# The order of row blocks in a whole-sum pass, and the place of its first eight rows

## The chip, the cores and the metric

The kernel runs on one core of one Trainium2 chip. A run's time is in device microseconds (us); lower is better. The kernel before was run three times. One more execution was taken with the hardware profiler, and all views of the profile come from it.

The engines are named by the profile's letters: PE is TensorE (PEld its weight loads), DVE is VectorE, ACT is ScalarE, POOL is GpSimd, and SP is the sync engine, whose queue issues most of the DMA transfers.

## The reference

The input is a feature matrix x of 2708 nodes by 128, and a 2708 by 2708 float32 matrix `adj`. Four layers follow, each of the form "layer norm of x plus a graph layer". Only the first two matter here:

```python
# layer 0
A_hat = adj + I;  d = A_hat.sum(1) ** -0.5
x = layernorm(x + (d[:, None] * A_hat * d[None, :]) @ x @ W.T + b)
# layer 1
XW = x @ W;  s_col = XW @ a[:f];  s_row = XW @ a[f:]
den = exp(leaky_relu(s_row[:, None] + s_col[None, :], 0.01))
num = adj @ den
att = where(num != 0, den / num, 0)
x = layernorm(x + adj @ (att @ XW))
```

The other two layers (a hyperbolic one, and one with the masks adj > 0 and adj < 0) come later and are not touched.

## The kernel before

The matrix comes in transposed, as `adjT`. It is cut into `NT` = 22 row tiles of 128 rows (the last has 20) and `NB` = 6 blocks of up to 512. Blocks 0 to 3 hold 4 tiles and 512 columns each; block 4 has 4 tiles too; block 5 has 2 tiles and 148 columns. A tile `A{d}_{c}` or `B{d}_{c}` holds row block d and column block c; a full one is 1 MB (1024 KB), one of the last column block 296 KB.

**Layer 0** streams all of adjT once as A tiles, adds up the degrees, and multiplies. Some tiles remain in SBUF (`kept`), in eleven "places" and some "thin" buffers for the narrow last column block. After the degrees, a loop over column blocks c = 0 to 4 finishes the layer. One pass of it issues, on TensorE, in a fixed order:

- `last_products`: the products with row blocks 4 and 5 for block c (`a`, L866; the unit matrix, L914), in three parts. Between the parts stand `norm_roots(c-1)` (the sums of squares, `var`, L251, then three ACT steps and DVE's split in three terms, `work`, L267) and `normed(c-1)` (a spread of the roots, `rs`, L273, then DVE's multiplication into `x`, L992).
- `projected(c-1)`: the products `xw` with the weights of layer 1 (L1001), then ACT copies `rc` and `xw`, and a store of `xw_d` on SP's queue (L1012).
- `degree_rows(c+1)`: `db`, L244, and ACT's copy.
- `summed_up(c)`: DVE adds up the block (L962, L963), ACT squares it (L965).
- `clamped(c-1)` and `count(c-1)`: DVE clamps the scores (`rcl`, L1019) and compares them with samples, eight `counts` (L1051) a full block, four for block 5. ACT also makes `e1`, the exponential of the score, from the clamped scores, block by block.

The same steps for blocks 4 and 5 follow after the loop; this is the tail of layer 0. `queued(engine)` ties each block of instructions behind the latest one queued on that engine, so the written order is kept there.

**The sort before layer 1.** Layer 1's numerators aren't computed as one large product: nodes are sorted into groups by score, and the numerator of a group is the one before it, changed by the nodes of that group. The stage needs `below` (sums of the counts, L1190), three transposes `prev_ps` (L1223), 26 DVE steps `jk` that follow each other (L1239), six broadcasts `rb` (L238) with ACT's `q_b`, the matmuls `low` (L1288, L1298), and two lists (`ohs` on DVE, L1326, `list` on PE, L1328). POOL then gathers rows of adjT (`rows_g`, L1415), and the attention loop begins (`num`, L1464).

**The whole-sum pass.** The first numerator is the sum over all rows k of e1[k] times row k of adjT. `whole_sum(n)` does the next n row tiles of it ("rows" from here on) into two PSUM banks (`t`, L803; the accumulators are `tot`). A row is nine matmuls with one output partition each, 18 records in the trace, over four column groups:

```python
sums_of = [(c, 0, BW, 32 * c, 0, 0) for c in range(4)]
sums_of += [(4, i * q4, min(BW, (i + 1) * q4), 32 * i, 1, 0) for i in range(4)]
sums_of += [(5, 0, width(5), 96, 1, BW - 3 * q4)]
```

Row blocks 4 and 5 are still in SBUF from layer 0. Row blocks 0 to 3 are fetched again, as B tiles, in that order: `fetch_next()` issues the loads on SP's queue (L824) for as long as `free_places` has a place. Seven places are free at first, which serves block 0 (places 6, 9, 3, 7 and 10) and B1_0 and B1_1 (place 1, and a buffer in `ut`). When the last row of a block has been summed, its places go back to the list and `fetch_next()` is called again. The thin buffer of B2_5 is that of A4_5, so this load must wait for block 4's rows in any case.

The rows were taken in the block order 0, 4, 5, 1, 2, 3. They were issued by calls of `sum_rows(n)`: four of them in the tail of layer 0, ten around `prev_ps` and `rb`, two ahead of the first list and one each at its steps 8 and 16, two ahead of the second list. At the end ACT copies the totals into `carry0`, two rows that POOL cleared before (L1166), in a region that the xw_d stores read.

Of the kernel before, what the change touches and what calls it, by code (L numbers as in the profile page):

```python
# [25 lines left out]
NB = (N + BW - 1) // BW  # L26
# [18 lines left out]
def rows(t):  # L45
    return min(P, N - t * P)


def width(b):
    return min(BW, N - b * BW)  # L50


def tiles(b):
    return range(b * (BW // P), min(NT, (b + 1) * (BW // P)))
# [3 lines left out]
def kernel(  # L58
# [20 lines left out]
    nc = tc.nc  # L79
# [98 lines left out]
    def acc_tile(b, name):  # L178
        return psum.tile([P, BW], F32, tag=f"acc{b}", name=name)

    def ps_tile(name):
        return psum.tile([P, BW], F32, tag="ps", name=name, bufs=2)
# [24 lines left out]
    def bslice(b):  # L207
        return slice(b * BW, b * BW + width(b))
# [555 lines left out]
    def fetch_next():  # L764

        while True:
            if not waiting:
                waiting.extend(itertools.islice(fetches, 1))
            if not waiting:
                return  # L770
            d, c = waiting[0]
            if c == NB - 1:
                t = thin_place((0, 1, 2, 0)[d], f"B{d}_{c}")
            elif free_places:
                held.setdefault(d, []).append(free_places.pop(0))
                t = big_place(held[d][-1], f"B{d}_{c}")
            else:
                return
            waiting.pop()
            kept[d, c] = fill_tile(t, d, c)  # L780
# [4 lines left out]
    e1 = c_tile("e1")  # L785
    e2 = c_tile("e2")
    q4 = (N - 4 * BW) // 4
    order = [0, NB - 2, NB - 1, *range(1, NB - 2)]
    steps = iter([(d, i) for d in order for i in range(len(tiles(d)))])

    sums_of = [(c, 0, BW, 32 * c, 0, 0) for c in range(4)]
# [4 lines left out]
    def whole_sum(n):  # L796
        if not tot:
            tot.extend(acc_tile(i, f"t1_{i}") for i in range(2))
        for d, i in itertools.islice(steps, n):
            k = tiles(d)[i]  # L800
            kw = rows(k)
            for c, a, b, o, bank, at in sums_of:
                last = nc.tensor.matmul(  # L803
                    tot[bank][o : o + 1, at : at + b - a],
                    lhsT=e1[:kw, k : k + 1],
                    rhs=kept[d, c][:kw, i, a:b],

                    start=(k == 0 and at == 0),
                    stop=(d == order[-1] and i == 3),
                    skip_group_check=True,  # L810
                )
            if i == len(tiles(d)) - 1:
                if d == NB - 2:
                    free_places.extend([4, 8, 0, 5, 2])
                elif d < NB - 2:
                    free_places.extend(held.pop(d))
                fetch_next()
        return last

    def fill_tile(t, d, c):  # L820
        w = width(c)
# [19 lines left out]
    with tc.tile_pool(name="tri", bufs=1) as tp:  # L841
# [115 lines left out]
        def summed_up(c):  # L957

            w, cs = width(c), bslice(c)
            dw, s, sq = (works[c][:, i, :w] for i in range(3))  # L960
            with queued(DVE):
                nc.vector.tensor_mul(s, acc[c][:, :w], dw)  # L962
                nc.vector.scalar_tensor_tensor(s, s, b0_s, x[:, cs], op0=ALU.add, op1=ALU.add)  # L963
            with queued(ACT):
                nc.scalar.activation(sq, s, AF.Square)  # L965
# [94 lines left out]

        def sum_rows(n):
            with queued(PE):
                return whole_sum(n)

        scaled = None

# [60 lines left out]
        for c in range(NB - 1):  # L1127
            for part in range(3):
                last_products(c, part)
                if c and part == 0:  # L1130
                    norm_roots(c - 1)
                    if c > 1:
                        count(c - 2, 4, 7)
                elif c and part == 1:
                    normed(c - 1)
                    if c > 1:
                        count(c - 2, 7)
            if c:
                projected(c - 1)
                degree_rows(c + 1)  # L1140
            summed_up(c)
            if c:
                clamped(c - 1)
                count(c - 1, 0, 4 if c < NB - 2 else 1)
# [2 lines left out]
        count(NB - 3, 1, 3)  # L1147
        norm_roots(NB - 2)
        norm_roots(NB - 1)
        sum_rows(1)  # L1150
        count(NB - 3, 3, 6)
        normed(NB - 2)
        sum_rows(1)
# [1 line left out]
        count(NB - 3, 6)  # L1155
        projected(NB - 2)
        projected(NB - 1)
        sum_rows(2)
        clamped(NB - 2)
        count(NB - 2)  # L1160
        clamped(NB - 1)
# [6 lines left out]
    with ctx_keep:  # L1168
# [11 lines left out]
        with tc.tile_pool(name="sort", bufs=1) as st_p:  # L1180
# [36 lines left out]
                    )  # L1217
            nc.vector.tensor_tensor(prev[:, 0, :], prev[:, 0, :], prev[:, 1, :], op=ALU.max)
            prev_ps = ps_tile("prev_ps")
            sum_rows(2)  # L1220
            with queued(PE):
                for q in range(len(SAMPLES)):
                    nc.tensor.transpose(  # L1223
# [1 line left out]
                    )  # L1225
            for b in range(NB):
                w, cs = width(b), bslice(b)
                sum_rows(3 if b < 2 else 1)
                with queued(PE):
                    pr = bcast_block(rcl[:, 0, :], b, f"rb{b}")  # L1230
                with queued(ACT):
                    nc.scalar.activation(q_b[:, cs], pr[:, :w], AF.Exp, scale=0.99)
# [75 lines left out]
            for i in range(2):  # L1308
                for n in range(3):
                    nc.vector.tensor_mul(  # L1310
                        val[i][:, :, 2 + n, :], oh[i], terms[:, n, i, :].unsqueeze(2).to_broadcast(grid)
                    )
                for h, (ta, tb) in enumerate(((0, t_a), (t_a, NT))):
                    nn = (tb - ta) * GM
                    nc.vector.tensor_mul(
                        pos[i][:, ta:tb, :], low[i, h][:, :nn].rearrange("p (t g) -> p t g", g=GM), oh[i][:, ta:tb, :]
                    )
                nc.vector.tensor_reduce(slot[:, i, :], pos[i], AX.X, ALU.add)
                nc.vector.tensor_scalar(slot[:, i, :], slot[:, i, :], 2.0, None, op0=ALU.add)
                ps = ps_tile(f"list{i}")  # L1320
                sum_rows(2)
                for t in range(NT):
                    if i == 0 and t in (8, 16):
                        sum_rows(1)
                    ohs = srt([P, P], f"ohs{i}_{t}", BF16, 10, "ohs")
                    nc.vector.tensor_scalar(ohs, iota_b, slot[:, i, t : t + 1], None, op0=ALU.is_equal)  # L1326
                    with queued(PE):
                        nc.tensor.matmul(  # L1328
                            ps[:, : 6 * GM],
                            lhsT=ohs,  # L1330
                            rhs=val[i][:, t, :, :].rearrange("p n g -> p (n g)"),
                            start=(t == 0),
                            stop=(t == NT - 1),
                        )
                lists.append(ps[:, : 6 * GM].rearrange("p (n g) -> p n g", g=GM))
                li = srt([P, 6, GM], f"list_s{i}")
                nc.vector.tensor_copy(li, lists[i])
                node, value, occ = li[:, 0, :], li[:, 2, :], li[:, 5, :]
                nc.vector.scalar_tensor_tensor(node, node, float(P), li[:, 1, :], op0=ALU.mult, op1=ALU.add)
                if i == 0:  # L1340
                    for h in range(2):
                        fi = srt([P, GM], f"fi{h}", F32, 2, "fi")
                        nc.vector.tensor_scalar(fi, node, 2.0, float(h), op0=ALU.mult, op1=ALU.add)
                        nc.vector.tensor_scalar(row_i[:, h, :], fi, 0.0, float(2 * N - 1), op0=ALU.max, op1=ALU.min)
                else:
                    nc.vector.tensor_scalar(inval, occ, -1.0, 1.0, op0=ALU.mult, op1=ALU.add)
                    nc.vector.scalar_tensor_tensor(node, inval, float(N), node, op0=ALU.mult, op1=ALU.add)
                    nc.vector.tensor_scalar(xw_i, node, 0.0, float(N), op0=ALU.max, op1=ALU.min)

                nc.vector.tensor_add(value, value, li[:, 3, :])  # L1350
                nc.vector.tensor_add(value, value, li[:, 4, :])
                mask = srt([P, GM], f"mask{i}")
                nc.vector.tensor_scalar(mask, occ, -EMPTY, EMPTY, op0=ALU.mult, op1=ALU.add)
                nc.vector.tensor_add(value, value, mask)
                if i == 0:
                    nc.scalar.activation(e1_l, value, AF.Exp)
                    nc.scalar.activation(e2_l, value, AF.Exp, scale=0.01)
                else:
                    nc.scalar.activation(gj_l, value, AF.Exp, scale=0.99)
                    nc.vector.tensor_copy(occ_l, occ)  # L1360

                    nc.vector.tensor_scalar(inval, inval, 1.0e-18, None, op0=ALU.max)
# [615 lines left out]
```

## Time and profile before

| | us |
|---|---|
| median of 3 runs (lowest, highest) | 903.19 (901.72, 904.63) |
| the profiled execution | 905.07 |
| its span, first to last instruction | 903.4 |
| PE busy | 847.1 |
| DVE busy | 554.8 |
| ACT busy | 389.0 |
| POOL busy | 206.1 |

The span is what the instruction records cover; 1.67 us of the profiled execution lie outside it. The granted TensorE clock had a mean of 0.973 of full speed. An engine's busy time says how much it did, not what the end waited for: this is told by the chain of waits, by the timeline of a stretch, and by the table of windows (busy time, granted clock and DMA rate in a stretch). Times in a timeline count from the span's start.

### The profile page before, as it was taken

To read this page: it belongs to the slowest core of one execution; us is meant where nothing else is said; L and a number is where in the kernel's file an instruction comes from. 1 tells how busy PE (TensorE), PEld (TensorE's weight loads), DVE (VectorE), ACT (ScalarE), POOL (GpSimd) and SP (SyncE) were. 2 spreads that over 40 slices of the span, in tenths; PEclk is the share of its full clock that TensorE was granted. 3 is DMA by queue.
4 is the path that set the end of the run, shared out by engine and by line. 5 is a ranking of instruction groups with operands and counts; after the bars stand their busy time and mean duration, and the time that the engine had idled before them with its cause. 6 is when DMAs were issued, how large, how long until landed. Compare 5 with 4: busy or idle time off the path is not lost.

```text
span 903.4 us, 9470 instructions
## 1 busy us (share of the span) xinstructions
PE 847.1 (94%) x3268; PEld 429.5 (48%) x3268; DVE 554.8 (61%) x1189; ACT 389.0 (43%) x681; POOL 206.1 (23%) x176
## 2 busy tenths in 40 slices
PE   3699999699899999999999999989999899999996
PEld 3244454335344445444454444534444555555555
DVE  4777548988788888889971226375644564233313
ACT  3776433215787777787761115273332221000000
POOL 5221000101788885776500000000000000000000
PEclk9799999989899999999999999999999999999997
DMA  9995684596596555445534776496764565474410
GB/s 341 366 361 204 120 245 144 182 383 215 180 372 213 151 162 158 142 153 154 154 122 168 266 268 229 134 335 238 265 222 132 210 211 198 145 253 142 160 42 19
DMA packets 95979, 184.30 MB, mean 204 GB/s; under 512 B 6446, under 2 KB 23551, under 8 KB 95668
## 3 DMA queue, kind: packets, MB, share of 16 engines
q1 hardware_dynamic: 85700, 143.82, 46.2%
q0 software_dynamic: 8352, 37.76, 13.0%
q10 hardware_dynamic: 1872, 2.04, 0.7%
q8 instruction: 28, 0.46, 0.2%
q14 instruction: 27, 0.22, 0.1%
HBM read 179.33 MB, written 4.28 MB: 203 GB/s over the span
## 4 chain that ended last, share of the span: by engine, by line
PE 84%; DMA 8%; DVE 5%; ACT 2%; issue 1%; SPq 0%; DVEq 0%; ACTq 0%
PE a L1588 22%; PE num L1464 13%; PE uacc L1491 13%; PE a L1867 12%; PE a L866 10%; PE a L1876 6%; DMA A<-in_adjT_dram 4%; DMA B<-in_adjT_dram 3%; PE t L803 1%; DMA cb<-in_adjT_dram 1%; PE pp L1825 1%; DVE counts L1051 1%; PE mx L1695 1%; PE su L251 0%; DVE work L267 0%
## 5 line engine op out<-in xcount | busy, mean ns | idle before, releaser
L1415 POOL DMA_INDIRECT rows_g<-in_adjT_dram,row_i x52 | 131.2, 2523 | 90.6 <-PE num L1464 40.9
L1469 ACT ACTIVATE ln<-num,inval,occ_l 128x512 f32<-128x512 f32 x156 | 107.5, 725 | 52.7 <-DVE rows_g L1467 48.7
L1867 PE MATMUL a<-cb,ut 128*128 128x512 f32 (+2 forms) x264 | 125.8, 559 | 1.3 <-DMA cb<-in_adjT_dram 1.3
L1491 PE MATMUL uacc<-att,xw_g 128*128 128x512 f32 (+1 forms) x312 | 126.3, 542 | 0.0
L1876 PE MATMUL a<-mask,node 128*128 128x512 f32 (+2 forms) x264 | 120.3, 537 | 0.7 <-DVE mask L1855 0.7
L1464 PE MATMUL num<-rows_g,w_all 128*128 128x512 f32 (+1 forms) x276 | 113.6, 544 | 0.8 <-ACT ln L1469 0.8
L1588 PE MATMUL a<-cb,q_b 128*128 128x512 f32 (+2 forms) x264 | 111.7, 561 | 1.8 <-DMA cb<-in_adjT_dram 1.8
L866 PE MATMUL a<-A,q_b 128*128 128x512 f32 (+2 forms) x264 | 106.1, 549 | 1.5 <-DMA A<-in_adjT_dram 1.5
L1588 PE MATMUL a<-cb,xw 128*128 128x512 f32 (+2 forms) x264 | 107.3, 550 | 0.0
L1467 DVE COPY rows_g<-num 2x512 f32<-2x512 f32 x150 | 88.0, 612 | 15.8 <-PE num L1464 14.6
L1491 PEld LDWEIGHTS uacc<-att,xw_g 128*128 128x128 f32 x312 | 59.1, 190 | 59.1 <-issue 50.0
L1483 DVE TENSOR_TENSOR att<-att,ln 128x1354 f32<-128x1354 f32 x52 | 80.5, 1548 | 2.0 <-ACT ln L1479 2.0
L1464 PEld LDWEIGHTS num<-rows_g,w_all 128*128 128x128 f32 x276 | 49.8, 190 | 53.8 <-issue 39.6
L1876 PEld LDWEIGHTS a<-mask,node 128*128 128x128 f32 (+1 forms) x264 | 48.5, 193 | 49.4 <-issue 47.6
L230 ACT ACTIVATE sq_l<-s 128x512 f32<-128x512 f32 (+1 forms) x11 | 6.6, 604 | 148.4 <-DVE s L1885 116.7
L1479 ACT ACTIVATE ln<-ln 128x1354 f32<-128x1354 f32 x52 | 69.3, 1333 | 1.7
L1855 DVE TENSOR_SCALAR mask<-cb 128x3072 fp32r<-128x3072 f32 (+5 forms) x24 | 33.5, 1395 | 59.3 <-PE a L1876 58.6
L866 PEld LDWEIGHTS a<-A,q_b 128*128 128x128 f32 (+1 forms) x264 | 45.9, 191 | 50.0 <-issue 46.7
L1588 PEld LDWEIGHTS a<-cb,q_b 128*128 128x128 f32 (+1 forms) x264 | 45.1, 192 | 46.9 <-issue 42.8
L1588 PEld LDWEIGHTS a<-cb,xw 128*128 128x128 f32 (+1 forms) x264 | 45.1, 190 | 46.5 <-issue 46.5
L1074 ACT ACTIVATE xw<-A 128x2048 f32<-128x2048 f32 (+3 forms) x36 | 57.0, 1582 | 8.3 <-DMA b_s<-in_b_dram 4.4
L1456 DVE TENSOR_SCALAR att<-q_b,gj_l 128x1354 f32<-128x1354 f32 x52 | 48.2, 927 | 12.6 <-PE uacc L1491 12.5
(445 smaller groups left out, 899.5 us busy)
## 6 DMA issues: line engine op xcount, KB each, us to landing
cb<-in_adjT_dram SPq DMA_DIRECT2D x15, 2816.0 KB
cb<-in_adjT_dram SPq DMA_DIRECT2D x15, 2560.0 KB
A<-in_adjT_dram SPq DMA_DIRECT2D x25, 1024.0 KB
B<-in_adjT_dram SPq DMA_DIRECT2D x18, 1024.0 KB
cb<-in_adjT_dram SPq DMA_DIRECT2D x3, 814.0 KB
cb<-in_adjT_dram SPq DMA_DIRECT2D x3, 740.0 KB
ut<-in_adjT_dram SPq DMA_DIRECT2D x2, 1024.0 KB
A<-in_adjT_dram SPq DMA_DIRECT2D x5, 296.0 KB
```

Of the source, the lines that this page charges most:

```text
L866: nc.tensor.matmul(acc[c][:, :w], lhsT=z[:kw, k, :], rhs=t[:kw, i, :w], start=c not in begun, stop=(d == NB - 1 and k == NT - 1), skip_gro ...
L1074: checks[d, c] = nc.scalar.activation(below[:, :nt, :w], t[:, :nt, :w], AF.Relu, scale=-1.0, accum_out=neg_sum[:, NB * c + d : NB * c + d ...
L1415: got = nc.gpsimd.indirect_dma_start(out=gat[q], out_offset=None, in_=adj_h, in_offset=bass.IndirectOffsetOnAxis(ap=row_i[:, h, g : g + 1] ...
L1464: nc.tensor.matmul(num[:, : cb - ca], lhsT=w, rhs=gat[q][:, ca:cb], start=True, stop=True)
L1467: nc.vector.tensor_copy(gat[q + 1][0:2, ca:cb], num[0:2, : cb - ca])
L1469: nc.scalar.activation(ln_n[q][:, ca:cb], num[:, : cb - ca], AF.Ln, scale=occ_l[:, g : g + 1], bias=inval[:, g : g + 1],)
L1479: nc.scalar.activation(ln_n[q], ln_n[q], AF.Exp, scale=-1.0)
L1483: nc.vector.tensor_mul(att[q], att[q], ln_n[q])
L1491: nc.tensor.matmul(uacc[h][c][:, : cb - ca], lhsT=xw_g[:, g, :], rhs=att[q][:, ca:cb], start=(g == 0), stop=(g == GM - 1),)
L1588: nc.tensor.matmul(acc[:, :w], lhsT=weights[:kw, k, :], rhs=pc[:kw, t, :w], start=(k == 0), stop=(k == NT - 1),)
L1867: nc.tensor.matmul(acc[:, :w], lhsT=edge[:ke, k, :], rhs=pc[:ke, t, :w], start=(k == 0), stop=False, skip_group_check=True,)
L1876: nc.tensor.matmul(acc[:, :w], lhsT=node[:kw, k, j, :], rhs=mask[:kw, t - ma, :w], start=False, stop=(k == NT - 1 and j == 1), skip_group_ ...
```

## The change

The order of row blocks becomes 0, 1, 4, 5, 2, 3. The places of block 1 are thus given back before those of block 4, and the later loads take other places and follow in another order. The calls of `sum_rows` are set anew: two rows each in the passes c = 3 and c = 4 of the loop (all of block 0), right behind `degree_rows(c+1)` on TensorE's queue; two, one and one in the tail (all of block 1); one ahead of `prev_ps` and eight in the first four `rb` steps (block 4, block 5, three rows of block 2); three ahead of the first list, and one each at its steps 8 and 16 (the last of block 2, and block 3); none ahead of the second list. `whole_sum` no longer returns its last instruction, which no caller used.

```diff
-    order = [0, NB - 2, NB - 1, *range(1, NB - 2)]
+    order = [0, 1, NB - 2, NB - 1, *range(2, NB - 2)]
...
-                last = nc.tensor.matmul(
+                nc.tensor.matmul(
...
-        return last
...
-                return whole_sum(n)
+                whole_sum(n)
...
             summed_up(c)
+            if c in (NB - 3, NB - 2):
+                sum_rows(2)
             if c:
                 clamped(c - 1)
...
         norm_roots(NB - 1)
-        sum_rows(1)
+        sum_rows(2)
         count(NB - 3, 3, 6)
         normed(NB - 2)
         sum_rows(1)
...
         projected(NB - 1)
-        sum_rows(2)
+        sum_rows(1)
         clamped(NB - 2)
...
             prev_ps = ps_tile("prev_ps")
-            sum_rows(2)
+            sum_rows(1)
...
-                sum_rows(3 if b < 2 else 1)
+                sum_rows(2 if b < 4 else 0)
...
                 ps = ps_tile(f"list{i}")
-                sum_rows(2)
+                sum_rows(3 if i == 0 else 0)
```

In the order that the build gives the instructions, TensorE has the rows at the places named. SP's queue issues B1_2, B1_3, B1_4, B2_0 and B2_1 ahead of the last two xw_d stores; then B2_2, B2_3 (in `ut`), B2_4, B3_0, B3_1, B2_5 and the rest of block 3; the store of `x_d` (L1518, 1408 KB), which stood ahead of these loads, comes last. On POOL the clearing of `carry0` comes ahead of the four small `terms` steps, which stood before it. On ACT `e1_l` comes behind six of the nine copies into `carry0`, and on DVE the copy of `carry0` into the first gathered rows comes ahead of the two copies into `w_all`.

## The prediction

> **What bounds the kernel now.** I read the page first: engine shares and the chain that ended last.
>
> ```profile
> PE 847.1 (94%) x3268; PEld 429.5 (48%) x3268; DVE 554.8 (61%) x1189; ACT 389.0 (43%) x681; POOL 206.1 (23%) x176
> PE 84%; DMA 8%; DVE 5%; ACT 2%; issue 1%; SPq 0%; DVEq 0%; ACTq 0%
> ```
>
> TensorE bounds the kernel as a whole, but the edit lies between 150 and 225 us, so that stretch decides. TensorE's timeline there (start, duration, instruction, idle before it):
>
> ```profile
> 150.65 1.16 PE L1001 MATMUL xw<-w1ext,x 128*128 128x130 f32 x8
> 151.65 0.60 PE L244 MATMUL db<-ident,dcol 128*128 128x128 f32 x4
> 152.09 1.06 PE L914 MATMUL a<-ident,q_b 128*128 128x128 f32 x8
> ...
> 157.43 0.40 PE L273 MATMUL rs<-work,sel 128*128 128x128 bf16 x4 [0.29 <-DVE work L267]
> ...
> 165.75 0.40 PE L273 MATMUL rs<-work,sel 128*128 128x128 bf16 x4 [0.43 <-DVE work L267]
> 166.08 1.34 PE L803 MATMUL t<-B,e 128*1 128x512 f32 x18
> 167.35 0.28 PE L273 MATMUL rs<-work,sel 64*128 64x128 bf16 x2
> 168.88 1.61 PE L1001 MATMUL xw<-w1ext,x 128*128 128x130 f32 x12 [1.24 <-DVE x L992]
> 170.42 2.50 PE L803 MATMUL t<-B,e 128*1 128x512 f32 x36
> 177.61 0.48 PE L1190 MATMUL below<-counts,ones_b 128*128 128x384 bf16 x1 [4.69 <-DVE counts L1051]
> ```
>
> Two regimes. In the block loop (143.5 to 161.0) TensorE is busy 16.92 of 17.5 us (window table), and the gaps of 0.29 wait for VectorE work that TensorE's own earlier "var" matmul started: a TensorE loop. After 163 VectorE rules: the sum rows (L803) fill waits, and TensorE idles 4.69 us for the counts. Four rows there cost nothing today.
>
> Then the waits, and SP's timeline:
>
> ```profile
> PE below L1190 <- DVE counts L1051: 4.7, 1, 4.7
> PE t L803 <- DMA B<-in_adjT_dram: 2.2, 2, 1.7
> SPq L824 <- PE t L803: 7.9, 2, 7.3
> ```
> ```profile
> 169.07 0.33 SPq L1518 DMA_DIRECT2D x_d<-x  x1
> 170.54 1.77 SPq L1012 DMA_DIRECT2D xw_d<-xw  x2
> 172.60 24.06 SPq L824 DMA_DIRECT2D B<-in_adjT_dram  x12
> ```
>
> The next B loads leave at 172.60, once row block 0 is summed and its places are free. From the window table (start:end, length, busy time of PE, PEld, DVE, ACT, POOL, granted clock, DMA share, GB/s):
>
> ```profile
> 143.50:152.00 8.50, 8.21 (x42) 3.95 (x41) 7.88 (x26) 3.39 (x13) 0.19 (x1) 1.00 0.11 34
> 182.00:183.00 1.00, 1.00 (x14) 0.20 (x6) 0.13 (x1) 0.00 (x0) 0.00 (x0) 0.50 1.01 381
> 184.00:188.00 4.00, 4.00 (x62) 1.92 (x58) 3.79 (x12) 0.09 (x1) 0.00 (x0) 1.00 1.05 384
> 200.00:201.00 1.00, 0.89 (x4) 0.40 (x5) 0.93 (x5) 0.00 (x0) 0.00 (x0) 0.54 1.06 389
> ```
>
> DMA is nearly idle to 168, then saturated at about 385 GB/s. TensorE's clock is half after each pause.
>
> **What the skill says.** The Trainium skill, "DMA: Bandwidth & Descriptors", section "Anatomy of one DMA": [...]semaphore waits hold the issuing sequencer. [...]B2_4 released TensorE at 199.15; it and all queued ahead (eight B loads of 1.049 MB, x_d 1.44 MB, xw_d 0.39 MB: 10.2 MB) had by the window table (10.9 MB moved from 168 to 199.1) passed 1.7 us earlier. "TensorE: Matmul & The Clock Gate", Part 1: an idle window of about 3.4 us halves the clock, as long a busy one restores it. Here idleness from 172.9 gave 0.60 in 176 to 177 and 0.50 until 183; even the 1.7 and 0.5 us waits around 198 to 200 gave 0.54. Same page, Part 3: small-M matmuls to different 32-column groups run concurrently. Here 18 records of up to 0.59 us make a row of 1.25.
>
> **The change, part by part.** *Unit.* A row is 18 records; two rows took 2.50 us at 170.42, hence 1.25 each at full clock; at half clock two took 178.61 to 183.16, 4.55.
>
> *Block 0's rows move into passes c = 3 and c = 4* (two each, behind "db", ahead of the next pass). The built order has them there. Their loads landed long before (DMA idle from 144), so no wait. But TensorE sets the pace there, and var, ACT's roots and L267 all follow behind: 2 x 2.5 = **+5.0 us** with no cover. The four rows taken out of the tail save nothing: they lay under VectorE.
>
> *Block 1's rows come into the tail, with their loads.* B1_2, B1_3 and B1_4 need places of block 0, freed by its last row. In pass 4 "db" was 160.71 to 160.93; shifted 2.5, rows 163.4 to 165.9, the last from 164.7, its first matmuls done near 165.6: the loads leave then, 7.0 earlier than before. But block 1's first row now stands right behind the second "var", which ended at 164.2, so 169.2 now. Three loads are 3.15 MB: at 385 GB/s 8.2 us, plus 2.2 fixed (1.7 measured after the bytes, about 0.5 before them: x_d, issued at 169.07, showed bytes before 170). B1_4 lands at **176.0**. B1_0 and B1_1 are there early; each later matmul stops for its load: a wait of up to 6.8 us in pieces.
>
> *Who stands behind it.* In TensorE's queue: normed(4)'s spread (rs), a row, normed(5)'s rs, projected(4), (5), the last row; behind those ACT's rc, VectorE's rcl and 12 counts, then "below". VectorE can do only three counts of block 3 meanwhile; the last two stand behind x. After landing, two rows owe ten narrow matmuls: 0.85 us at full, 1.7 at half clock. So rs starts at 176.9 to 177.7 against 165.75. From rs to rcl took 4.52 (165.75 to 170.27), about 2 of it VectorE's counts, done by now. In its place TensorE does rs 0.4, row 1.25, rs 0.28, then xw to rcl 1.4: 3.4, or 3.8 with VectorE's last two counts after x of block 5, at full clock; up to 6.0 with matmuls doubled. The clock should be half; I take 4.9. Rcl: 177.3 + 4.9 = 182.2 against 170.27, **+11.9** (both ends: +10.4 to +13.4). From rcl to "below" VectorE's 7.34 stays: below at 189.5.
>
> *What comes back.* One row instead of two ahead of prev_ps: it ran at 183.16 though VectorE was ready at 182.12, -1.0. Later, loads that start earlier against a chain 12 us later have landed: the 2.2 us of B waits go, and the lists have five rows, not six, none ahead of the second. The 26 jk steps (184.3 to 201.4) stay VectorE's, so only VectorE's idle gaps between 213 and 222.5 can close: 0.66 + 0.53 + 0.30 + 0.34 = 1.8. Together 1.0 to 2.8; I take **-2.0**.
>
> *At nothing.* SP: the xw_d stores of blocks 4 and 5 now stand behind five B loads, x_d behind all. They hold the carry0 memset (2.44 us) and POOL's terms, moved behind it; that is done near 190, needed near 213. B2_5 shares A4_5's buffer, so it and block 3's last loads wait for block 4: in by about 212, wanted near 219. Were these covers gone, each would cost a wait like the 2.2 above. ACT's carry copies and VectorE's carry copy swap places with e1_l and w_all, which have slack (first matmul 227.50, carry done 226.5). The dropped return value issues nothing. The attention loop and later layers shift whole.
>
> *Sum.* +11.9 - 2.0 = **+9.9 us**. The profiled execution took 905.07 (span 903.4, 1.67 around it), 1.9 above the median of 903.19; I add to the median: **913.1**. Ends: 10.4 - 2.8 = +7.6, 13.4 - 1.0 = +12.4.
>
> **Rivals.** *Loads in time.* If no row stops for a load, rs is late by 5.0 alone and the return is 2.0: 906.2. This needs 3.15 MB plus the fixed part in the 3.6 us between 165.6 and 169.2; the fastest microsecond shows 439 GB/s. Were block 1's places free earlier it would hold; they are not. 7%.
> *Faster.* The inserted rows hide: VectorE idles 1.35 us for ACT in pass 4, and if the loop's real bound were VectorE or ACT, +5.0 becomes 0; with loads in time, only the return stays, at its full 2.8: 900.4. It decides where rcl is late by less than 2.8 minus the 2.7 that 0.3% needs, so practically not at all. Against it: TensorE's 16.92 of 17.5 us and that the 1.35 wait starts from a TensorE matmul. 3%.
> *Longer.* Half clock holds through the tail and again through the lists (TensorE would idle before "low" with fewer rows), the return is lost: up to 13.4 + 2 for doubled matmuls in the lists, 918.6. For it: 0.54 after a mere 2 us pause. 10%.
> *It doesn't do what it says.* A scheduler could put the rows elsewhere; the built order shows them where the text puts them, so only its waits are open.
>
> **How the numbers follow.** My case has 80%: 910.8 to 915.6 by its ends, widened by about 2 for the landing estimate. The range 907.5 to 917.0 leaves out the first two rivals, most of the third, and a small part of mine: under 2 in 10. 0.3% (2.7 us) is about what a measurement of this kernel can tell from no change. Faster by more 3%; within 5% (half of the first rival and a little of mine); slower 92%.
>
> **What would show it.** Right: L803 rows near 152 and 163; a TensorE wait of about 6 us on B between 169 and 176, then clock 0.5; "below" near 189.5; no B wait after 195; everything from L1464 on as long as before. Wrong: "below" before 184 (loads were fast), or the list's end, 44.9 us after "below" today (177.61 to 222.46), unchanged or longer (no return).

## The result, and the profile after

The kernel before ran in 903.88 us here (median of 4 runs), the changed kernel in 912.26 us (median of 4, 911.88 to 916.96). The ratio is 1.0109, with a 95% interval of 1.0071 to 1.0146: 6.4 to 13.2 us slower. Run once more, beside other kernels, it took 914.37 us (median of 5) against 902.77 (ratio 1.0136, 1.0111 to 1.0161). The profiled execution took 916.96 us, the slowest of the four; its span is 915.2 us. The other three took 911.88 to 912.43.

Engine shares and the chain that ended last:

```profile
PE 850.1 (93%) x3268; PEld 429.9 (47%) x3268; DVE 555.8 (61%) x1189; ACT 389.1 (43%) x681; POOL 204.0 (22%) x176
PE 84%; DVE 7%; DMA 6%; ACT 2%; issue 1%; DVEq 0%; SPq 0%; ACTq 0%
```

The same instructions, 3268 matmuls as before; TensorE's busy time grew by 3.0 us of the 11.8 that the span grew, so most of the loss is idleness. Below, a part of TensorE's work is called cold where the granted clock was half, and warm where it was full. TensorE's timeline (start, duration, instruction, idle before it; "below" is L1191 now, line numbers move by one or two):

```profile
152.05 2.50 PE L803 MATMUL t<-B,e 128*1 128x512 f32 x36
159.92 0.40 PE L273 MATMUL rs<-work,sel 128*128 128x128 bf16 x4 [0.29 <-DVE work L267]
163.52 2.50 PE L803 MATMUL t<-B,e 128*1 128x512 f32 x36
168.90 0.41 PE L251 MATMUL var<-work,mean_w 128*32 128x128 f32 x4 [0.89 <-ACT work L964]
169.14 0.59 PE L803 MATMUL t<-B,e 128*1 128x512 f32 x1
...
170.99 1.02 PE L803 MATMUL t<-B,e 128*1 128x512 f32 x2 [0.82 <-DMA B<-in_adjT_dram]
173.69 0.90 PE L803 MATMUL t<-B,e 128*1 128x512 f32 x2 [1.68 <-DMA B<-in_adjT_dram]
...
174.41 3.43 PE L803 MATMUL t<-B,e 128*1 128x512 f32 x23
177.77 0.40 PE L273 MATMUL rs<-work,sel 128*128 128x128 bf16 x4
...
189.43 0.48 PE L1191 MATMUL below<-counts,ones_b 128*128 128x384 bf16 x1 [6.96 <-DVE counts L1050]
...
194.01 0.90 PE L1224 MATMUL prev_ps<-ident,prev 128*128 128x128 f32 x3 [1.14 <-DVE prev L1219]
```

Each pair of block 0's rows takes 2.50 us, and everything behind it moves by that: rs of pass 4 from 157.43 to 159.92, the second var from 163.78 to 168.90 (+5.1). Then two rows that need 2.50 us take from 169.14 to 177.77, 8.6 us: they stop for loads, and normed(4)'s rs comes 12.0 us later than in before (165.75). The waits (total, times, longest) and SP's timeline:

```profile
PE below L1191 <- DVE counts L1050: 7.0, 1, 7.0
PEld t L803 <- DMA B<-in_adjT_dram: 5.4, 3, 2.6
PE low L1289 <- DVE val L1278: 4.6, 1, 4.6
PE t L803 <- DMA B<-in_adjT_dram: 2.5, 2, 1.7
```
```profile
165.71 4.64 SPq L823 DMA_DIRECT2D B<-in_adjT_dram  x5
181.25 0.92 SPq L1011 DMA_DIRECT2D xw_d<-xw  x2
...
203.60 2.92 SPq L1519 DMA_DIRECT2D x_d<-x  x1
```

The loads leave at 165.71, before at 172.60. Part of the wait stands under PEld, since a weight load stops for the tile too; read both rows. No B wait is left after 195.

From "below" on, the two kernels run nearly alike: the lists end 44.6 us after "below" (before 44.9), the first num matmul comes 49.6 us after it (before 49.9), and the attention loop's last uacc matmul 246.4 us after that num (before 246.5). Behind the loop the two traces differ by 0.5 us (429.3 and 429.8). So in this trace the loss is made ahead of "below", and the return, the 2.0 us that I forecast to come back behind it, is missing.

### The profile page after: what moved, and what is told of

Read it like the earlier page. It is cut to its first block, busy times and chain, and to the rows that moved or that the text cites. A ratio compares the mean times of both kernels' runs of the same rounds, so it can differ in the third digit from the quotient of the medians.

```text
span 915.2 us, 9468 instructions
## 1 busy us (share of the span) xinstructions
PE 850.1 (93%) x3268; PEld 429.9 (47%) x3268; DVE 555.8 (61%) x1189; ACT 389.1 (43%) x681; POOL 204.0 (22%) x176
## 4 chain that ended last, share of the span: by engine, by line
PE 84%; DVE 7%; DMA 6%; ACT 2%; issue 1%; DVEq 0%; SPq 0%; ACTq 0%
PE a L1589 22%; PE num L1465 13%; PE uacc L1492 13%; PE a L1868 11%; PE a L865 9%; PE a L1877 6%; DMA A<-in_adjT_dram 4%; DVE jk L1240 2%; PE t L803 2%; DMA cb<-in_adjT_dram 1%; PE pp L1826 1%; DVE counts L1050 1%; DMA B<-in_adjT_dram 1%; PE low L1299 1%; PE mx L1696 1%
## 5 line engine op out<-in xcount | busy, mean ns | idle before, releaser
L1416 POOL DMA_INDIRECT rows_g<-in_adjT_dram,row_i x52 | 129.0, 2480 | 94.6 <-DVE ohs L1327 43.4
L1589 PEld LDWEIGHTS a<-cb,q_b 128*128 128x128 f32 (+1 forms) x264 | 45.1, 192 | 46.8 <-issue 42.8
```

Source lines behind the costliest of these rows:

```text
L1416: got = nc.gpsimd.indirect_dma_start(out=gat[q], out_offset=None, in_=adj_h, in_offset=bass.IndirectOffsetOnAxis(ap=row_i[:, h, g : g + 1] ...
L1589: nc.tensor.matmul(acc[:, :w], lhsT=weights[:kw, k, :], rhs=pc[:kw, t, :w], start=(k == 0), stop=(k == NT - 1),)
```

## The experiments

Three notes on reading. Traces start up to 2.2 us earlier or later than that of before, so positions are compared after taking off the difference at the xw matmul of pass 4 (159.72 in before, 2.50 more where two rows stand ahead of it). "Loop" is the time from the first num matmul to the end of the last uacc matmul. Positions and loops come from one traced execution of each kernel (two of the changed one), run times are medians: behind the loop, where no edit reaches, the traces took 425.7 to 429.8 us, so that the medians of few runs (4 to 8 of the changed kernel and of each variant of it) can't settle a difference of 1 or 2 us.

| kernel | below, later than before by | first num, later by | loop | run time against the runs of before taken beside it, us (ratio, 95% interval) |
|---|---|---|---|---|
| before | 0 | 0 | 246.5 | 0 |
| changed | 11.8 | 11.6 | 246.4 | +8.4 (1.0109, 1.0071 to 1.0146) |
| changed, again | 11.4 | 10.5 | 246.3 | +11.6 (1.0136, 1.0111 to 1.0161) |
| e1_rows_early | 6.1 | 4.0 | 246.6 | +4.5 (1.0049, 1.0031 to 1.0068) |
| e2_no_load_wait | 5.1 | 4.6 | 246.3 | +3.4 (1.0044, 1.0026 to 1.0061) |
| e4_order_only | 0.0 | 3.1 | 246.5 | +2.6 (1.0032, 1.0019 to 1.0045) |
| e5_wait_aside | 6.1 | 4.9 | 246.2 | +4.5 (1.0048, 1.0031 to 1.0066) |
| e3_warm_low | 11.6 | 10.0 | 248.1 | +8.3 (1.0095, 1.0069 to 1.0122) |
| e6_warm_filler | 11.4 | 10.8 | 246.3 | +9.2 (1.0098, 1.0077 to 1.0120) |
| e7_filler_and_rows_split | 11.5 | 9.6 | 248.0 | +10.6 (1.0120, 1.0096 to 1.0144) |
| e8_longer_filler | 11.5 | 9.4 | 248.0 | +8.6 (1.0093, 1.0068 to 1.0119) |
| v1_x_d_behind | 0.5 | -0.8 | 248.0 | +1.0 (1.0005, 0.9993 to 1.0016) |
| v2_rows_under_counts | 0.4 | -0.1 | 248.1 | +1.0 (1.0007, 0.9996 to 1.0018) |
| v3_warm_gb | 0.0 | -0.9 | 245.3 | -2.0 (0.9984, 0.9971 to 0.9996) |

The theory was: +5.0 for block 0's rows, uncovered in a loop that TensorE paces, and about 7 for a wait on loads with the tail's path queued behind it. The rivals: the rows hide; their place matters, not their loads; the traffic slows the tail.

**The first part alone** (before, with only block 0's rows moved):

```diff
+            if c in (NB - 3, NB - 2):
+                sum_rows(2)
...
-        sum_rows(1)
...
-        sum_rows(1)
...
-        sum_rows(2)
```

> The kernel before, with its own order of row blocks, and block 0's four rows in passes 3 and 4 (two each) in place of the three calls of the tail (1, 1 and 2 rows): the first part of the change alone, with no row of block 1 in the tail. My theory (the inserted rows lie uncovered in a loop that TensorE paces): normed(4)'s rs in the tail about 5.0 us later than 165.75, 'below' 4 to 5 us after the 177.61 of before, near 182; no wait on B ahead of it; the B loads leave near 165.6, so the later waits on B (2.2 us) shrink and 1 to 2.5 us come back. Total +2 to +4 us on before, about 906.5. Rival (the rows hide under the waits on VectorE and ScalarE): 'below' within 1 us of 177.6, total 0 to -2. Rival (the tail needs the rows to keep the clock up): 'below' at 184 or later with half clock ahead of it, total +5 or more.

Measured: "below" 6.1 us late, total +4.5. There is no B wait ahead of "below"; 1.5 us of B waits on PE remain (before 2.2). The rows do not hide. But 6.1 is more than the 4 to 5 of my theory, and 4.5 more than its 2 to 4; TensorE's timeline says why, and it goes toward the last reading, that the tail needs the rows to keep the clock up:

```profile
170.43 0.61 PE L273 MATMUL rs<-work,sel 128*128 128x128 bf16 x4 [1.56 <-DVE work L267]
...
173.55 2.97 PE L1001 MATMUL xw<-w1ext,x 128*128 128x130 f32 x12 [1.82 <-DVE x L992]
```

With the four rows gone from the tail, TensorE idles there, its clock is half from 169.5 to 186.6, and xw takes 2.97 instead of 1.61 us. The rows that "cost nothing" in the tail had kept the clock up; taking them out cost 1.0 (6.1 against the 5.1 of the next kernel).

Behind "below" 2.1 us come back, the 2.0 that I forecast for the changed kernel: the lists end 42.8 us after "below" (before 44.9) and num comes 47.8 us after it, with a loop of 246.6. "Low" is warm here, behind a pause of 1.58 us:

```profile
207.59 0.38 PE L1287 MATMUL low<-val,upper 128*128 128x494 bf16 x1 [1.58 <-DVE val L1276]
```

**The wait alone taken away.** The changed kernel, with one index changed:

```diff
-                    rhs=kept[d, c][:kw, i, a:b],
+                    rhs=kept[d, c if d != 1 or c == NB - 1 else c % 2][:kw, i, a:b],
```

> The changed kernel, but the rows of block 1 read column blocks 0 and 1 in the places of 2, 3 and 4, so every matmul of theirs reads a tile that landed long before; the number, size and place of the matmuls are the same, and the sums of row block 1 are other sums. My theory (the second half of the delay is the wait for B1_2 to B1_4): normed(4)'s rs near 171 instead of 177.77, 'below' near 182.5 to 184 instead of 189.43, and no wait on B in the tail; since the later stages are bound by VectorE and TensorE as in the changed kernel, the total falls by 4 to 7 us, to 905.5 to 908.5. Rival (the delay comes of the place of the rows, not of their loads): 'below' within 1 us of 189.4, total as the changed kernel. Rival (the loads' wait only hides another one): 'below' near 186, total -2 to -3.

```profile
171.21 0.40 PE L273 MATMUL rs<-work,sel 128*128 128x128 bf16 x4
...
182.41 0.48 PE L1191 MATMUL below<-counts,ones_b 128*128 128x384 bf16 x1 [5.85 <-DVE counts L1050]
```

In TensorE's timeline rs is at 171.21 instead of 177.77, 6.2 us earlier when the start of the trace is taken off, and "below" is 5.1 us late instead of 11.8: block 0's rows alone, to 0.1 us. The same matmuls stand in the same place, so the 6.2 are their loads (5.2 against the second trace of the changed kernel). The 6.7 at "below" are not the wait alone: the build of this kernel also put POOL's clearing of `carry0` behind its terms, as in before, and that is worth 1.1 of them (why, is told under "From rcl to "below"" further down), while the way from rs to rcl is 0.6 longer.

**The order alone** (an edit of before):

```diff
-    order = [0, NB - 2, NB - 1, *range(1, NB - 2)]
+    order = [0, 1, NB - 2, NB - 1, *range(2, NB - 2)]
```

> The kernel before with the order of row blocks alone changed to 0, 1, 4, 5, 2, 3; rows stay where they were. Theory (block 1's loads leave with block 0's last row, near 172.6, and the last of its three lands 8 to 10.5 us later, at 181 to 183): 'below' stays at 177.6; the first row of block 1 stands ahead of prev_ps, whose two rows wait on B until 181 to 183, so prev_ps runs at 184 to 186 instead of 183.16; from there VectorE waits for prev_ps; total +1 to +4 us, about 905.5. Rival (the order costs nothing: the loads are in before prev_ps is due): prev_ps within 0.5 us of 183.16, total within 1 us of before. Rival (later loads, now those of blocks 4, 5, 2, 3, come too late for the lists): a B wait after 195 longer than the 2.2 us of before, total above +4.

```profile
180.88 1.02 PE L803 MATMUL t<-B,e 128*1 128x512 f32 x2 [0.84 <-DMA B<-in_adjT_dram]
...
185.28 0.54 PE L1223 MATMUL prev_ps<-ident,prev 128*128 128x128 f32 x3
```

"Below" does not move; block 1's first rows, now ahead of prev_ps, stop for their loads. prev_ps runs at 185.28 in a trace that starts 1.0 us early, so 3.1 us later than before, and 3.1 arrives at num. The order costs by itself here, since block 1 comes right behind block 0, whose places its loads need.

**The wait put where nothing stands behind it.** The changed kernel, with the tail's rows in one place:

```diff
         norm_roots(NB - 1)
-        sum_rows(2)
...
         normed(NB - 2)
-        sum_rows(1)
...
         projected(NB - 1)
-        sum_rows(1)
+        sum_rows(4)
```

> The changed kernel with block 1's four rows of the tail all behind projected(5), instead of 2, 1 and 1 rows ahead of normed(4), normed(5) and behind projected(5): the same rows, the same loads and the same wait on B, but nothing of the path stands behind it. Theory (the wait costs by what is queued behind it on TensorE): the wait on B remains, to about 176, and the rows run from there to about 181 at half clock; normed(4)'s rs at 171 (with nothing to do ahead of it, at half clock), 'below' at 183.5 to 184.5 as in the kernel with only block 0's rows moved; total 4 to 5.5 us under the changed kernel, near 907.5. Rival (the loads' traffic itself slows the tail, through VectorE, ScalarE or POOL, or the rows end too late for 'below'): 'below' at 187 or later, total within 2 us of the changed kernel.

Measured: "below" 6.1 us late instead of 11.4 to 11.8, total 7.1 us under the changed kernel that ran beside it. One detail missed: there is no B wait at all. xw, at half clock again, ends at 177.95, and by then the loads have landed. So this is no wait with nothing behind it. But it is the same rows, loads and order, and "below" is as late as with block 0's rows alone (6.1 in e1): what block 1's rows cost was decided by where they stood in TensorE's queue. (Here too POOL's terms stand ahead of the clearing.)

**The missing return.** In the changed kernel TensorE idles ahead of "low" and then runs it cold:

```profile
214.17 0.57 PE L1289 MATMUL low<-val,upper 128*128 128x494 bf16 x1 [4.59 <-DVE val L1278]
214.53 3.87 PE L1299 MATMUL low<-val,ones_b 128*128 128x468 bf16 x18
```

Before, no pause stood ahead of them, and they were warm:

```profile
204.12 0.38 PE L1288 MATMUL low<-val,upper 128*128 128x494 bf16 x1
204.34 2.07 PE L1298 MATMUL low<-val,ones_b 128*128 128x468 bf16 x18
```

Four kernels try this; each is the changed kernel with one edit, or, in e7, with two.

e3: ten rows instead of eight in the rb steps, one instead of three ahead of the first list.

```diff
-                sum_rows(2 if b < 4 else 0)
+                sum_rows(2 if b < 4 else 1)
...
-                sum_rows(3 if i == 0 else 0)
+                sum_rows(1 if i == 0 else 0)
```

> The changed kernel, with ten instead of eight rows in the rb steps (2,2,2,2,1,1) and one instead of three ahead of the first list. Theory (the return that I forecast was given back because TensorE idles 4.6 us ahead of 'low', runs it at half clock, and then has three rows standing ahead of the first list): 'low' at full clock, its two groups about 2.1 instead of 4.4 us, the lists' end 42.5 to 43.5 us after 'below' instead of 44.6, total 1 to 2 us under the changed kernel. Rival (the lists' stretch is VectorE's either way): lists' end 44 to 45 us after 'below', no difference in the total. Rival (the two rows more delay the rb steps or meet a load that is not there): +1 to +2.

The lists end 43.4 us after "below", as the theory had it, but not for its whole reason: the second of the two extra rows met a B load that was not there (2.6 us), and low's first group was still 3.13 us long. The total against before (+8.3) is not below the changed kernel's.

e6, then e7 (e6 plus the rows 1 and 2 in place of 3 and 0), then e8 (38 in place of 26):

```diff
+                        for _ in range(26 if (i, h) == (0, 0) else 0):
+                            nc.tensor.transpose(low[i, h][:, :P], ident, ident)
```

> The changed kernel, with 26 transposes of ident (about 0.155 us each by the rb row, 4.0 us in all) written into low's own PSUM tile ahead of its first matmul, in the 4.6 to 6.0 us in which TensorE idles there; low's start flag overwrites them, no load and no VectorE work is added. Theory (half clock at 'low' took back what the chain from 'below' to 'low' had gained): low's first group 2.1 us instead of 3.6 to 3.9, the lists' end 42.3 to 43.3 us after 'below' instead of 44.6, the attention loop's first matmul about 48 us after 'below' instead of 49.0 to 49.6; total 1 to 2 us under the changed kernel, near 911. Rival (VectorE sets the lists' end, and the clock doesn't matter): 44 to 45 us after 'below', no difference. Rival (the fillers reach past the moment when val is ready): 'low' late by up to 1 us, nothing gained.

> The kernel of the run beside it, and of the five rows in the lists one ahead of the first list instead of three, and two ahead of the second instead of none (as the kernel before has them, less one). Theory (the stretch from low's end to the lists' end is TensorE's, and rows count by their number, not by their place): the lists' end within 0.7 us of that of the run beside it, the first list 2.5 us earlier, the second's wait for the carry copies of ScalarE (0.72) gone or moved. Rival (rows ahead of the first list delay VectorE's work behind it, that is a part of the lost return): lists' end 1 to 2 us earlier, total as much.

The filler took 3.0 us, not 4.0, and left 2.06 us idle in e6 and 1.90 in e7. Yet e6 was cold at "low" and e7 was not. Window rows (start:end, length, busy time of PE, PEld, DVE, ACT, POOL, clock, DMA share, GB/s) of e6, then of e7:

```profile
213.00:214.00 1.00, 0.39 (x2) 0.13 (x2) 0.96 (x3) 0.33 (x1) 0.00 (x0) 0.81 0.98 417
214.00:215.00 1.00, 1.00 (x4) 0.42 (x3) 1.00 (x3) 1.00 (x7) 0.00 (x0) 0.50 0.77 327
```
```profile
213.00:214.00 1.00, 0.00 (x0) 0.00 (x0) 0.96 (x3) 0.00 (x0) 0.00 (x0) 1.00 1.01 427
214.00:215.00 1.00, 0.94 (x5) 0.48 (x5) 1.00 (x3) 0.88 (x3) 0.00 (x0) 1.00 0.98 417
```

E7's lists end 43.1 us after "below", e6's 44.3: the 1.2 between them is the clock (low took 5.9 against 7.6 us), less 0.4 that the split of the rows lost. So rows count there by their number, not by their place, and the clock takes 1.6 us here, 1.9 in the changed kernel. The run times of both, +9.2 and +10.6, show no gain.

> The changed kernel with 38 filler transposes ahead of 'low' in place of 26, since 26 took 3.0 us instead of the 4.0 that I had reckoned (0.115 us each) and left 2 us idle: now 4.4 us, 0.7 us idle. Theory: 'low' is at full clock, wherever the clock's decisions fall, its first group 2.1 us; the lists' end 42.3 to 42.9 us after 'below', the attention loop's first matmul 47.4 to 48.0. Whether the total falls by these 1.8 us depends on the next pause, between the lists' end and the second batch of num: if it makes TensorE cold a second time, as in the kernels with the rows split and with x_d behind, the loop is 248 us long instead of 246.4 and the total is that of the changed kernel within 1 us; if not, 1.5 to 2 us under it. Rival (the filler itself delays 'low'): lists' end 44 us or more after 'below'.

With 0.77 us idle, low is warm (2.07), the lists end 42.8 us and num starts 47.8 us after "below": 1.8 us earlier than in the changed kernel, as forecast. The total is not lower, and in the trace the gain goes in the loop, which is 248.0 us long instead of 246.4. The traces of e3, e7, e8, v1 and v2 have this loop; all five reach num earlier than their neighbour. Their second batch of num matmuls is cold, as here in v1, where before it was warm behind a wait that was longer:

```profile
234.17 2.93 PE L1464 MATMUL num<-rows_g,samples 128*128 128x512 f32 x4 [1.98 <-ACT w_all L708]
```

```profile
234.84 1.68 PE L1464 MATMUL num<-rows_g,samples 128*128 128x512 f32 x4 [2.29 <-ACT w_all L708]
```

What was earned ahead of num, a cold num took back in these five. It does not have to be so: e1 had the warm "low" and the loop of 246.6, and kept its 2.1 us up to the loop's end.

**Versions of before.** v1 issues the x_d store behind the last B load, v2 adds rows in TensorE's pause ahead of "below" to v1:

```diff
-            nc.sync.dma_start(out=x_d, in_=x)
+            with tc.issue_after(fill_tile.last):
+                nc.sync.dma_start(out=x_d, in_=x)
```
```diff
         clamped(NB - 1)
+        sum_rows(3)
         count(NB - 1)
...
-            sum_rows(2)
+            sum_rows(1)
...
-                sum_rows(3 if b < 2 else 1)
+                sum_rows((3, 2, 1, 1, 1, 1)[b])
...
-                sum_rows(2)
+                sum_rows(2 - i)
```

> The kernel before with the 1.44 MB store x_d issued on SP behind the last B load instead of ahead of those that leave from 172.60. Theory: every B load of that stretch lands 1.44 MB / 385 GB/s = 3.7 us earlier, the waits on B at 199 and 200 (1.7 and 0.5 us) vanish, and TensorE is not cold behind them; 'below' at 177.6 as before; total -0.5 to -2 us, about 902.8. Rival (those waits are hidden under VectorE's 26 jk steps): 0. Rival (x_d is then late for what reads it): +1 or more.

> The kernel of the run beside it (x_d behind), and three rows of row block 4, which has long been in SBUF, in the 4.7 us in which TensorE idles ahead of 'below'; one row instead of two ahead of prev_ps, then 3, 2, 1, 1, 1, 1 rows in the rb steps and five instead of six in the lists. Theory: 'below' stays at 177.6 with the clock full where it was half, prev_ps 1.0 us earlier at 182.1, the lists' gaps of up to 1.8 us in part closed; total -1.5 to -3.5 us on before, about 901.5. Rival (TensorE is not on the path there, VectorE is): -0.5 to -1 or none. Rival (the rows run at half clock, 2.3 us each, and reach past 177.6): 'below' 1 to 3 us late, total +1 to +3.

Neither gains. In v1 the B waits on PE fell from 2.2 to 1.3 us and num came 0.8 earlier, and the loop took it back. In v2 prev_ps was 0.7 earlier (1.0 expected), but the rows reached block 1 sooner than its loads (B waits on PE 3.6 us), and the loop was the long one too. "Below" was 0.5 and 0.4 us late where no delay was expected. In both builds POOL's clearing of `carry0` had moved ahead of the terms, and block 5's rcl took 0.65 us instead of 0.17 (in v1; POOL's and VectorE's timelines, then VectorE's in before):

```profile
173.07 2.44 POOL L1166 MEMSET xw<- 2x2816 f32 x1 [22.39 <-DMA xw_d<-xw]
```
```profile
174.88 0.65 DVE L1019 TENSOR_SCALAR rcl<-rc 128x4 f32<-128x4 f32 x1
```
```profile
175.00 0.17 DVE L1019 TENSOR_SCALAR rcl<-rc 128x4 f32<-128x4 f32 x1
```

v3 is before with filler transposes ahead of the first gb:

```diff
+            warm = ps_tile("warm")
+            with queued(PE):
+                for _ in range(14):
+                    nc.tensor.transpose(warm[:, :P], ident, ident)
             for g in range(FIRST):
                 group_matrix(w_first, g)
```

> The kernel before, with 14 filler transposes of ident into a PSUM tile of their own between the second list and the first gb (1.6 us, in the 1.7 us in which TensorE idles from 222.46). Theory (the clock falls to half at 224.0 for 6.8 us because of this pause, and holds up gb and the first six num matmuls): full clock from 224 to 231, num's six in 2.5 instead of 4.1 us, the loop's end 1 to 2 us earlier, total -1 to -2 us, about 902.3: a version that beats both. Rival (the loop's start waits for ScalarE's w_all and the rows that POOL fetches, not for TensorE): num faster, but the loop's end within 0.5 us, total unchanged. Rival (filler late or clock still falls): 0 to +1.

```profile
221.72 1.69 PE L1371 MATMUL warm<-ident 128*128 128x128 f32 x14
...
226.36 2.45 PE L1468 MATMUL num<-rows_g,samples 128*128 128x512 f32 x6
```

In before:

```profile
227.50 4.08 PE L1464 MATMUL num<-rows_g,samples 128*128 128x512 f32 x6
```

Num's first six took 2.45 instead of 4.08 us, the clock stayed at 1.00 from 221 to 250, and the loop ended 2.2 us earlier. The total is 1.4 us lower by the ratio (0.4 to 2.6), 2.0 by the medians: a version that beats both kernels, if only just, by useless matmuls in a pause.

> The changed kernel once more, beside the kernels of this call, so that they can be compared on one chip. Its first four runs had a median 8.4 us over before (interval 6.4 to 13.2), its profiled execution was 11.9 over the profiled execution of before. If the 8.4 is the better figure, 911.5 to 913.5 here; if the profiled execution is, 914 to 917. Either way 'below' is near 189.4, the lists' end about 44.6 us after it, and the first matmul of the attention loop about 11.6 us later than in before.

The changed kernel came out at +11.6; the two figures, 8.4 and 11.6, hold the forecast 9.9 between them, and no run tells which is nearer. Its two traced executions differ by 6.1 us in their span (915.2 and 909.1), and 4.1 of them lie behind the loop (429.8 and 425.7 us), in the same instructions. TensorE's clock was at half there for 17.8 us in the first and 10.4 in the second. One such place, window rows of the first trace and then of the second:

```profile
608.00:610.00 2.00, 2.00 (x5) 0.97 (x4) 1.38 (x10) 1.01 (x2) 0.00 (x0) 0.50 1.04 384
```
```profile
590.00:615.00 25.00, 20.91 (x101) 13.04 (x100) 16.70 (x104) 15.10 (x38) 0.00 (x0) 1.00 0.98 352
```

## Why the prediction was right, and which of its terms were not

The mechanism of the loss held, and so did the total; the return behind "below" did not come. The sum had four wrong sizes: rs came 0.5 us later than taken, the way from rs to rcl was 1.7 shorter, that from rcl to "below" 1.1 longer, and the return 1.7 smaller. By the first trace the sum should have been +11.6 at num, not +9.9. That the forecast of "below" was met to 0.1 us is luck, as the first three of these sizes nearly cancel; and that the first median, +8.4, lies below the forecast is no sign of the return, which the traces do not have.

- **Block 0's rows, +5.0.** Right: 2.50 and 2.50 in the passes, +5.1 at "below" in e2. That the four rows taken out of the tail "save nothing" was right too, but it was half the matter: e1 shows that their absence costs 1.0 by the clock. In the changed kernel block 1's rows stand there, so it doesn't show.
- **The loads.** Right: they left at 165.71 (165.6 forecast), rs ran at 177.77 (176.9 to 177.7), in the second trace 1.0 earlier. The rows' delay, 8.6 less 2.5 or 6.1 us in all, came in pieces, as was forecast: TensorE stood idle for 2.5 of it, and the rest went in waits under PEld and in matmuls at half clock. That clock was half only from 174 to 177, as the window table has it:

```profile
174.00:175.00 1.00, 1.00 (x8) 0.13 (x1) 0.00 (x0) 0.00 (x0) 0.00 (x0) 0.50 1.03 379
...
177.00:178.00 1.00, 1.00 (x22) 0.58 (x17) 0.00 (x0) 0.00 (x0) 0.00 (x0) 0.87 1.05 389
```

- **From rs to rcl, 4.9 taken.** Measured 3.2 (177.77 to 181.00). I had taken the middle between full and half clock up to rcl; it was 0.87 in 177 to 178 and full after. "TensorE's clock is half after each pause" was too simple a reading: in before, xw is warm behind a pause of 1.24 us (168.88), and num behind one of 2.29.
- **From rcl to "below", 7.34 kept.** Measured 8.43. This is the "at nothing" paragraph: I noted that the carry0 memset on POOL was released by the later xw_d stores and moved ahead of the terms, and gave it no cost. Timelines of POOL and of VectorE in the changed kernel:

```profile
184.53 2.44 POOL L1167 MEMSET xw<- 2x2816 f32 x1 [33.84 <-DMA xw_d<-xw]
```
```profile
185.73 1.27 DVE L1018 TENSOR_SCALAR rcl<-rc 128x4 f32<-128x4 f32 x1
```

  Block 5's rcl, 0.17 us in before, takes 1.27 and ends with the memset (186.97 and 187.00). In all eight traces in which the memset stands ahead of the terms (the two of the changed kernel, e3, e6, e7, e8, v1, v2) this rcl takes 0.65 to 1.92 us and ends within 0.05 us of the memset; in before, e1, e2, e4, e5 and v3, where the memset stands behind, it takes 0.17. The Trainium skill, "SBUF — State Buffer", section "SBUF: two separate sides", describes this: VectorE (in some of its modes) and GpSimd share a port pair by an exclusive lock, and the later one blocks. The counts beside the memset kept their 0.61. That the lock is the cause is argued from this pattern; no run moved the memset by itself. The nearest to it is v1, which has the rows of before: 0.5 us longer in rcl, and "below" 0.5 us late. With rs 0.5 late, -1.7 and +1.1, "below" came at 189.43 against 189.5 forecast.
- **The return, 2.0 taken.** Measured 0.2 at the lists' end, 0.3 at num (0.9 at num in the second trace of the changed kernel). Prev_ps came 1.0 earlier behind "below", as forecast (before had two rows ahead of it and ten in the rb steps, twelve in all), and low started 1.8 earlier (24.74 against 26.51 us after "below"). Then low, begun at half clock, took 7.9 us instead of 6.0: 1.9 of the gain went there, and the lists gave 0.4. Where low was warm, in e1, the return was 2.1; with low cold and no wait on loads, in e2, it was 0.5. The prediction's own test, the lists' end 44.9 us after "below" as today, said "no return", and that is what it shows. The rival "longer" had this very mechanism ("TensorE would idle before "low" with fewer rows") and gave it 10%; I kept the two apart where they belonged together. Here the chain to "low" became VectorE's, TensorE stood idle for 4.59 us, and then it started cold.
- **The rivals.** "Loads in time" is refuted by the trace and priced by e2: it would have been +3.4, where the prediction gave it +3.0 (906.2). "Faster" falls with e1.

What stays open: why the two measurements of the changed kernel differ by 3.2 us. Their traces differ by 1.1 at num, and the other way round, and the loops are alike. The 4.1 us between the same two traces behind the loop, where the clock fell at other times, are large enough for it; that the medians differ for this reason is not shown.

## What to carry to other kernels

Before moving work ahead of a wait on one queue, ask what stands behind it: the same rows with the same loads made "below" 5.3 to 5.8 us later in front of the path than behind it (e5; 1.1 and 1.7 of it are the longer rcl beside POOL's memset). A load whose buffer was freed by the last step came too late for the next one (e4, +3.1), so put resident data between them in the order. And count a gain ahead of a TensorE pause only after looking at the clock behind the pause: it went back there in the changed kernel ("low") and in e8 (num), and it stayed in e1.

## What the runs showed of the hardware

- **The clock changes on a fixed grid.** In the window tables the mean clock of the microsecond in which it changes gives the moment (0.70 in 211 to 212: a fall at 211.40). The clock fell at 211.40 and 235.28 in the changed kernel and rose again at 218.24 and 242.12: 23.88 and 6.84 us, or 7 and 2 times 3.41. In e6, falls at 186.30 and 213.62 are 8 times 3.41 apart. The Trainium skill, "TensorE: Matmul & The Clock Gate", Part 1, gives a free-running window of 3413 ns, and the traces agree. But no idle window is needed: in e6 the window 210.21 to 213.62 held 1.35 us of TensorE work and the clock fell; in e7 the window 210.99 to 214.40 (placed by its changes at 187.10 and 197.34) held 1.51 and it did not. Nor is busy time the measure: in the changed kernel the window 231.87 to 235.29, with matmuls of the second list, held 2.08 us, and the clock fell. What of the work counts stays open. So a pause of about 2 us was free (1.90 in e7, 2.29 in before) or cost 1.6 us (2.06 in e6) by where it fell, and a shift of less than 1 us went with the change from one to the other (num 0.8 earlier in v1). That is how the loop is 246.4 or 248.0 us long with the same instructions. Nor does the grid start with the kernel: in the two traces of the changed kernel the clock falls in the tail at 173.84 (0.92 in 173 to 174) and at 168.28 (0.64 in 168 to 169; 169.15 with the start taken off), 4.7 us apart, which is no multiple of 3.41.
- **A memset of two partitions on POOL seems to hold a VectorE instruction of four values per partition for up to 1.75 us** (1.92 in e8 against 0.17; 0.65 in v1), while the counts beside it ran at their usual length.
- **A transpose of 128x128 float32 takes 0.115 us in a long row of its kind** (3.00 us for 26 in e6), where I had reckoned 0.155 from the rb row of four.
